# Query projection, load order and attention step order of a four-layer Perceiver kernel

## The chip, the cores and the metric

The kernel runs on one core of one Trainium2 chip. The metric is the device time of one execution in microseconds (us); the time shown for a kernel is the median of its runs.

The core's engines are named as in the profile: PE is TensorE (matrix products, into PSUM), DVE is VectorE, ACT is ScalarE, POOL is GpSimd and SP is SyncE, which here issues all loads. Each engine works through its own instructions in order.

## The reference

The model keeps a stream `x` of 2 x 256 tokens of width 256, and a context `ctx` of 2 x 4096 tokens of width 256 with a key mask. It runs eleven blocks, each on the layer norm of the stream and added to it:

```python
x = x + L0_xattn(layernorm(x), ctx, mask)   # 16 heads of 16, biases on q, k and v
x = x + L0_attn(layernorm(x))               # latent attention, 16 heads of 64, rotary
x = x + L0_ffn(layernorm(x))                # quantized, with a convolution of 3
x = x + L1_xattn(layernorm(x), ctx, mask)   # 16 heads of 16
x = x + L1_attn(layernorm(x))               # 16 heads of 16, over the stream itself
x = x + L1_ffn(layernorm(x))                # 16 experts, the best two
x = x + L2_xattn(ctx, layernorm(x))
x = x + L2_attn(layernorm(x))               # causal, gated
x = x + L2_ffn(layernorm(x))
x = x + L3_xattn(layernorm(x), ctx, ctx)    # linear attention with ranked features
x = x + L3_attn(layernorm(x))               # 16 heads of 16, in a window of 128
x = x + L3_ffn(layernorm(x))                # two layers
```

Four of these are touched: the two context attentions (`L0_xattn`, `L1_xattn`) and the two small attentions with heads of 16 (`L1_attn`, `L3_attn`). Such an attention is

```python
q, k, v = heads(h @ Wq + bq), heads(c @ Wk + bk), heads(c @ Wv + bv)
a = softmax(where(mask, -inf, q @ k.T) / 4)      # the scale differs by block
x = x + merge(a @ v) @ Wo
```

## The kernel before

Everything is kept transposed: features lie on the 128 partitions, and the 512 tokens along the row. A head of 16 takes 32 partitions (16 of its own, a row for the shift of the softmax, a row for the mask and empty ones), so a chunk of 128 partitions holds four heads, the 16 heads are four chunks `c`, and a *unit* is a chunk of one batch. There are eight units in an attention, with 256 queries each.

**PSUM.** A stage opens a pool of eight banks of 128 x 512 (`banks`, `stage`): by default two single ones called `mm`, two pairs called `sc` and two called `acc`. Both kinds of attention work with another split: one `mm`, three `sc` pairs, one `acc`. A tag with one buffer is given out again when its last reader is done.

**Start.** `constants` loads the vectors (biases and scales), `perceiver` loads x, and `context_constants` loads the mask, turns it into two rows of offsets that go to DRAM (`key_masks`), and computes `alive` (which batches have any unmasked key) with two products on PE. The weights of the first block, the features' weights and the first pair of context chunks (`ctx_k`) follow in the order of the code. SP issues these loads in the order that the scheduler gives them.

**Queries of a context attention** (`attend_to_context`, `take_queries`, `take`). The stream is centred (`xc`), four chunks are projected with `project`, which takes an `mm` bank for each; in between `measure` and `widen` make the reciprocal deviation of each token and spread it over all partitions (`wide`). For each chunk and batch DVE multiplies the projection by `wide` (L840) and adds the bias, in layer 1 also a factor 0 or 1 (L842, L844). Then the bank pool is changed and the attention starts. In it, step g computes first scores for unit g // 16 (L1113, L1121 takes their maxima), and later scores, exponentials and weighted sums (L1137, L1147, L1161), with projections of keys and values and the features of the last layer filled in by `plan`. In these two attentions the order of PE, DVE and ACT is written out by hand (`manual_schedule`); POOL and SP are ordered by the scheduler. The key tiles are filled with ones, since their mask and shift rows have to hold them; the value tiles `xv` too (POOL, L1071).

**A small attention** (`SmallAttention.attend`, L1405 on) does, in each step i, these things in order: sums and reciprocals of unit i-4 (`inverses`), the tops of unit i-1 transposed and added to its queries (`shift_queries`), first scores of unit i, weighted values of unit i-3 (`weigh`), second scores of unit i-1 (`scores`), and the product with the spread reciprocals of unit i-4 (`normalize`, by `to_heads`). Sums, tops and spread reciprocals (`den`) take turns in the one `mm` bank:

```python
if 0 <= i - 4 < n:
    self.inverses = self.net.inverses(self.weighed[i - 4])
if 0 <= i - 1 < n:
    self.shift_queries(i - 1)
if i < n:
    self.first_scores(i)
if 0 <= i - 3 < n:
    self.weigh(i - 3)
if 0 <= i - 1 < n:
    self.scores(i - 1)
if 0 <= i - 4 < n:
    self.normalize(i - 4)
```

Of the kernel before, what the change touches and what calls it, by code (L numbers as in the profile page):

```python
# [19 lines left out]
F32 = mybir.dt.float32  # L20
# [50 lines left out]
class Net:  # L71
# [87 lines left out]
    def constants(self):  # L159
        nc, const = self.nc, self.const  # L160
        c = lambda shape, name, dtype=F32: const.tile(shape, dtype, name=name, tag=name)
        self.vectors = c([P, sum(int(np.prod(v)) for v in VECTORS.values())], "vectors")
        nc.sync.dma_start(out=self.vectors, in_=self.ins["vectors"])
# [31 lines left out]
    def inverses(self, a):  # L195

        ps = self.mm("sums")
        for qt in range(2):
            self.matmuls(ps[:, qt * NG : (qt + 1) * NG], [(a[:, qt * P : (qt + 1) * P], self.den)])
        r = self.small.tile([P, 2, NG], F32, tag="inverses", name="inverses", bufs=2)  # L200
        self.nc.vector.reciprocal(r, ps[:, : 2 * NG].rearrange("p (q g) -> p q g", g=NG))
        return r

    def to_heads(self, r):

        ps = self.mm("den")
# [230 lines left out]
    def context_attention(self, x, q_bias, k_bias, v_bias, wq, wk, wv, wo, layer, alive=None, block=None):  # L437
# [11 lines left out]
        with tc.tile_pool(name="xa", bufs=1, reuse_waits="tile") as big, tc.tile_pool(name="xa_ctx", bufs=2, reuse_waits="tile") as cpool:  # L449
            a = ContextAttention(self, layer, big, cpool, (wk, k_bias), (wv, v_bias))  # L450
# [24 lines left out]
    def context_constants(self):  # L475
# [9 lines left out]
        with self.banks(), self.tc.tile_pool(name="mask", bufs=1, reuse_waits="tile") as tmp:  # L485
# [9 lines left out]
            most = tmp.tile([NR, 1], F32, name="mask_most", tag="mask_most")  # L495
            nc.vector.tensor_reduce(most, mf, AX.X, ALU.max)
            rows = tmp.tile([NR, NB, P], F32, name="batch_rows", tag="batch_rows")
            nc.gpsimd.memset(rows, 1.0)
            for b in range(NB):
                for sign, base in ((1, -b * NKC), (-1, b * NKC + NKC - 1)):  # L500
                    nc.gpsimd.affine_select(
                        out=rows[:, b, :],
                        in_=rows[:, b, :],
                        pattern=[[0, P]],
                        compare_op=ALU.is_ge,
                        fill=0.0,
                        base=base,
                        channel_multiplier=sign,
                    )
            self.alive = c([P, NB], "alive")  # L510
            ps = self.mm("alive_ps")
            for b in range(NB):
                nc.tensor.matmul(ps[:, b : b + 1], lhsT=rows[:, b, :], rhs=most, start=True, stop=True)
            nc.vector.tensor_scalar_min(self.alive, ps[:, :NB], 1.0)
# [265 lines left out]
class ContextAttention:  # L780
# [11 lines left out]
    def __init__(self, net, layer, big, cpool, keys, values):  # L792
        self.net, self.nc, self.layer, self.cpool = net, net.nc, layer, cpool
        (self.wk, self.k_bias), (self.wv, self.v_bias) = keys, values
        tile = lambda shape, name: big.tile(shape, F32, name=f"xa_{name}", tag=name)
        self.q = [tile([P, S], f"q{u}") for u in range(len(self.UNITS))]
# [4 lines left out]
        if layer == 0:  # L801
            for t in self.key_tiles:
                self.nc.gpsimd.memset(t, 1.0)
# [6 lines left out]

    def begin(self, n):

        self.begun = n
        if self.layer > 0:
            for t in self.key_tiles:
                self.nc.scalar.copy(t, self.net.ones[:, 0:1].to_broadcast([P, KC]))
            yield
# [4 lines left out]
    def take_queries(self, norm, wq, q_bias, alive):  # L822
        net = self.net
        for c in range(NC16):
            ps = net.project(wq, norm.chunks, c)
            if c == 0:
                net.measure(norm)
                waiting = ps
                continue
            if c == 1:  # L830
                wide = net.widened(norm.rstd)
                self.take(0, waiting, wide, q_bias, alive)
            self.take(c, ps, wide, q_bias, alive)

    def take(self, c, ps, wide, q_bias, alive):

        nc = self.nc
        for b in range(NB):
            q, at = self.q[b * NC16 + c], slice(b * S, (b + 1) * S)
            nc.vector.tensor_tensor(q, ps[:, at], wide[:, at], ALU.mult)  # L840
            if alive is None:
                nc.vector.tensor_scalar_add(q, q, q_bias[:, c : c + 1])  # L842
            else:
                nc.vector.tensor_scalar(q, q, q_bias[:, c : c + 1], alive[:, b : b + 1], ALU.add, ALU.mult)  # L844
# [131 lines left out]
    def attend(self, vpool, ppool, fpool):  # L976
# [12 lines left out]
        for g in range((n + 1) * PER + LAG + 2):  # L989
# [3 lines left out]
            run(self.beginning)  # L993
            run(fills.get(g, ()))
# [179 lines left out]
def l0_xattn(net, x):  # L1174
    wq, wk = net.load("L0x_wq", "L0x_wk")
    wv, wo = net.load("L0x_wv", "L0x_wo")
    qb, kb, vb = net.vec("L0x_qb"), net.vec("L0x_kb"), net.vec("L0x_vb")
    return net.context_attention(x, qb, kb, vb, wq, wk, wv, wo, 0)


def l0_attn(net, x):
# [9 lines left out]
    with tc.tile_pool(name="l0a", bufs=1, reuse_waits="tile") as big, tc.tile_pool(name="l0a_w", bufs=2, reuse_waits="tile") as work:  # L1191
# [36 lines left out]
        oT = big.tile([P, NCH, T], F32, name="oT", tag="oT")  # L1228

# [83 lines left out]
def l0_ffn_and_l1_xattn(net, x):  # L1313
# [4 lines left out]
        x, qb, None, None, wq, wk, wv, wo, 1, net.alive, block=lambda *of: l0_ffn(net, *of)  # L1318
# [17 lines left out]
class SmallAttention:  # L1336
# [68 lines left out]
    def attend(self):  # L1405
        n = len(self.UNITS)
        for i in range(n + 4):
            if 0 <= i - 4 < n:
                self.inverses = self.net.inverses(self.weighed[i - 4])
            if 0 <= i - 1 < n:  # L1410
                self.shift_queries(i - 1)
            if i < n:
                self.first_scores(i)
            if 0 <= i - 3 < n:
                self.weigh(i - 3)
            if 0 <= i - 1 < n:
# [911 lines left out]
```

## Time and profile before

| | before |
|---|---|
| median of 3 runs | 2512.33 us (2512.18 to 2951.45) |
| profiled execution | 2515.34 us, of which the span is 2513.4 us |
| granted PE clock in it | 0.958 |
| busy in the span | PE 93%, DVE 62%, ACT 43%, POOL 13% |
| loaded from DRAM | 154.25 MB |
| first small attention | about 1645 to 1704 us of the span |
| second small attention | about 2190 to 2244 us |
| context attention of layer 0, first scores | at 32.9 us |
| context attention of layer 1, first scores | at 957.6 us |

A row of the timeline gives start, duration, engine, line and operation (out <- in, sizes, how often), and in brackets how long the engine was idle before it and what ended that. A row of the chain gives start, length and owner of a piece of the work that ended last. `L180` is the helper behind most products, so its rows are told apart by the tiles' names. In the windows, the columns after the stretch are its length, the busy time and count of PE, PE's weight loads, DVE, ACT and POOL, then the granted clock, the share of the DMA engines and GB/s.

### The profile page before, as it was taken

How to read it: one execution, taken by the hardware profiler on the slowest of the kernel's cores; microseconds unless marked ns; L12 is line 12 of the kernel's file. 1: busy time of each engine (PE TensorE's matmuls, PEld its weight loads, DVE VectorE, ACT ScalarE, POOL GpSimd, SP SyncE). 2: the span in 40 equal slices, each digit the busy share in tenths (PEclk: the TensorE clock that was granted, in tenths of full speed). 3: DMA queues.
4: the chain of work that ended last, by engine and by line, in shares of the span. 5: the costliest groups of instructions: out<-in, count | busy, mean ns of one | idle time of the engine just before them, and what ended most of it. 6: DMA issues, size and time to landing. Idle time of an engine off the chain costs nothing.

```text
span 2513.4 us, 42846 instructions
## 1 busy us (share of the span) xinstructions
PE 2336.0 (93%) x17142; PEld 1252.9 (50%) x17142; DVE 1549.4 (62%) x2719; ACT 1093.2 (43%) x1917; POOL 333.2 (13%) x505
## 2 busy tenths in 40 slices
PE   7999999999999689999999999989999996889998
PEld 3455455544544364554454544554448453455454
DVE  4878888788736757877878778443241354334343
ACT  2456555555615333555555565531131252123232
POOL 3000001000024602000010000000011031002120
PEclk9999999999989799999999999989999997798989
DMA  5432232132010133322222220201232100100100
GB/s 185 138 105 86 88 96 94 52 111 64 10 38 35 48 103 108 101 91 90 90 94 86 77 98 28 83 14 43 96 100 93 43 18 14 34 21 12 58 12 21
DMA packets 97798, 174.42 MB, mean 69 GB/s; under 512 B 15120, under 2 KB 63888, under 8 KB 96704
## 3 DMA queue, kind: packets, MB, share of 16 engines
q1 hardware_dynamic: 97600, 171.68, 21.1%
q8 instruction: 136, 2.23, 0.4%
q14 instruction: 62, 0.51, 0.1%
HBM read 154.25 MB, written 0.59 MB: 62 GB/s over the span
## 4 chain that ended last, share of the span: by engine, by line
PE 57%; DVE 6%; ACT 2%; issue 1%; POOL 0%; DMA 0%; SPq 0%; ACTq 0%; DVEq 0%; POOLq 0%
PE s L1113 6%; PE s L1137 5%; PE proj L180 5%; PE attn_acc L1161 5%; PE v_ps L180 4%; PE expert L180 2%; PE k_ps L1034 2%; PE s L180 2%; PE c_acc L1753 2%; PE s L1430 2%; PE ffn_ps L180 2%; DVE mx L1121 2%; PE scores L342 1%; PE f_ps L180 1%; PE kc_sum L180 1%; PE qk_ps L180 1%
## 5 line engine op out<-in xcount | busy, mean ns | idle before, releaser
L1121 DVE TENSOR_REDUCE mx<-s 128x2 f32<-128x1024 f32 x512 | 603.2, 1221 | 224.6 <-PE s L1113 221.8
L1147 ACT ACTIVATE p<-s 128x1024 f32<-128x1024 f32 x512 | 496.0, 1021 | 255.8 <-PE s L1137 253.8
L1137 PE MATMUL s<-xa_q,xa_k 32*128 32x256 f32 x4096 | 342.3, 403 | 26.0 <-DVE mx L1121 23.0
L1113 PE MATMUL s<-xa_k,xa_q 32*128 32x512 f32 x2048 | 338.7, 642 | 7.0 <-ACT p L1147 2.3
L1137 PEld LDWEIGHTS s<-xa_q,xa_k 32*128 32x128 f32 x4096 | 212.7, 184 | 167.5 <-issue 92.6
L1161 PE MATMUL attn_acc<-p,xv 128*32 128x256 f32 x4096 | 276.2, 386 | 0.7 <-ACT p L1147 0.7
L1113 PEld LDWEIGHTS s<-xa_k,xa_q 32*128 32x128 f32 x2048 | 111.4, 183 | 124.7 <-issue 60.6
L667 DVE TENSOR_TENSOR ge<-fy 128x960 bf16<-128x960 f32 (+14 forms) x240 | 169.5, 706 | 6.5
L1161 PEld LDWEIGHTS attn_acc<-p,xv 128*32 128x32 f32 x4096 | 107.4, 109 | 131.4 <-issue 84.4
L621 POOL TENSOR_TENSOR fy<-fy,low 128x256 f32<-128x256 f32 x64 | 46.4, 725 | 881.3 <-ACT fy L620 881.1
L669 DVE TENSOR_TENSOR rank<-rank,ge 128x960 bf16<-128x960 bf16 (+14 forms) x240 | 104.2, 434 | 6.0
L671 DVE TENSOR_TENSOR rank<-rank,ge 128x960 bf16<-128x960 bf16 (+14 forms) x240 | 100.8, 420 | 2.6
L387 POOL TENSOR_SCALAR p<-p,r 128x128 f32<-128x128 f32 (+1 forms) x192 | 82.6, 442 | 127.0 <-DVE r L383 72.4
L1081 ACT COPY xv<-v_ps 128x512 f32<-128x512 f32 x64 | 37.6, 587 | 135.7 <-PE v_ps L180 135.7
L368 ACT ACTIVATE p<-p,top 128x256 f32<-128x256 f32 (+1 forms) x128 | 57.1, 447 | 66.6 <-DVE top L356 65.3
L180 PE MATMUL f_ps<-f_wk,f_ctx 128*128 128x256 f32 x256 | 68.9, 400 | 0.6 <-DMA f_ctx<-in_ctxT 0.6
L1034 PE MATMUL k_ps<-ctx_k,w_L0x_wq 128*64 128x512 f32 x256 | 66.0, 612 | 3.2 <-DMA ctx_k<-in_ctxT 2.9
L180 PE MATMUL v_ps<-w_L0x_wv,ctx_v 128*128 128x256 f32 x256 | 65.6, 400 | 0.8 <-ACT k_dense L1047 0.8
L180 PEld LDWEIGHTS f_ps<-f_wk,f_ctx 128*128 128x128 f32 x256 | 44.4, 189 | 43.3 <-issue 26.5
L1753 PE MATMUL c_acc<-pT,ctx_n 128*128 128x256 f32 x256 | 62.0, 387 | 4.2 <-ACT pT L1726 3.0
L180 PE MATMUL kc_sum<-f_tok,fy 128*128 128x257 f32 x256 | 64.2, 393 | 0.0
L180 PE MATMUL v_ps<-w_L1x_wv,ctx_v 128*128 128x256 f32 x256 | 63.8, 392 | 0.0
(478 smaller groups left out, 3366.8 us busy)
## 6 DMA issues: line engine op xcount, KB each, us to landing
ctx_k<-in_ctxT SPq DMA_DIRECT2D x128, 512.0 KB
ctx_v<-in_ctxT SPq DMA_DIRECT2D x64, 256.0 KB
xa_k<-k_dense SPq DMA_DIRECT2D x512, 32.0 KB
f_ctx<-in_ctxT SPq DMA_DIRECT2D x32, 256.0 KB
f_tok<-in_ctx SPq DMA_DIRECT2D x16, 512.0 KB
ctxT<-in_ctxT SPq DMA_DIRECT2D x16, 512.0 KB
ctx_n<-in_ctx SPq DMA_DIRECT2D x16, 512.0 KB
xa_k<-key_masks SPq DMA_DIRECT2D x128, 8.0 KB
```

The lines of the kernel that those rows point to most:

```text
L180: self.nc.tensor.matmul(out, lhsT=lhsT, rhs=rhs, start=i == 0, stop=i == len(pairs) - 1)
L387: nc.gpsimd.tensor_scalar(p[:, j, :nk], p[:, j, :nk], r[:, j : j + 1], 1.0, ALU.mult, ALU.mult)
L667: nc.vector.tensor_tensor(ge[:, :, :n], w[:, :, :n], w[:, :, P - n :], ALU.is_ge)
L669: nc.vector.tensor_tensor(rank[:, :, P - n :], rank[:, :, P - n :], ge[:, :, :n], ALU.add)
L671: nc.vector.tensor_tensor(rank[:, :, :n], rank[:, :, :n], ge[:, :, :n], ALU.subtract)
L1034: nc.tensor.matmul(ps[i * HR : (i + 1) * HR, :], lhsT=self.wk[:, d, c * HR : (c + 1) * HR], rhs=ctx[:, d, :], start=d == 0, stop=d == ND - 1,)
L1113: nc.tensor.matmul(pairs[i // 2][:, i % 2, :], lhsT=self.q[u][rows, qt * P : (qt + 1) * P], rhs=k[rows, :], start=True, stop=True,)
L1121: nc.vector.tensor_reduce(mx[:, qt, 2 * i : 2 * i + 2, kc], sc, AX.X, ALU.max)
L1137: nc.tensor.matmul(pairs[i // 2][:, i % 2, kk * S : (kk + 1) * S], lhsT=k[rows, at], rhs=self.q[u][rows, :], start=True, stop=True,)
L1147: nc.scalar.activation(p, sc, AF.Exp, scale=DH**-0.5)
L1161: nc.tensor.matmul(self.acc[i * HP : (i + 1) * HP, :S], lhsT=v[:, 2 * k2 + kk, at : at + HP], rhs=ps[i // 2][:, i % 2, kk * S : (kk + 1) * S],
L1753: nc.tensor.matmul(accs[m], lhsT=of[:, (k + i) % (KC // P), m * P : (m + 1) * P], rhs=pT[:, i, :], start=k + i == 0, stop=k + i == KT - 1,)
```

## The change

Three things change.

**Loads.** x is loaded first, then wk and wq, then the first pair of context chunks; the vectors, the mask, the features' weights and wv and wo follow. `alive` is found in the first self-attention block, not at the start. Four of the fourteen key tiles of layer 0 are filled by ACT at the start, and the other ten by POOL, as they are reached.

**Queries.** The four projections get banks of their own: two `mm` and the two halves of an `sc` pair. DVE finishes only unit 0. ACT copies the others out of PSUM as they are, and POOL multiplies them by `wide` and adds the bias, unit g at step g of the attention, while the scores of unit 0 run.

**Small attentions.** Tops and spread reciprocals share one bank, `aux`, half each, and the sums go into the second half of the bank of the weighted values, `acc`. The sums of unit i-3 come at the end of step i, and the product of unit i-4 before the second scores of unit i-1.

```diff
     def constants(self):
+        self.x = self.new_x()
+        nc.sync.dma_start(out=self.x, in_=self.ins["xT"])
         self.vectors = c([P, sum(int(np.prod(v)) for v in VECTORS.values())], "vectors")
-        nc.sync.dma_start(out=self.vectors, in_=self.ins["vectors"])
...
-    def inverses(self, a):
+    def inverses(self, a, ps=None):
-        ps = self.mm("sums")
+        ps = self.mm("sums") if ps is None else ps
...
-    def to_heads(self, r):
+    def to_heads(self, r, ps=None):
-        ps = self.mm("den")
+        ps = self.mm("den") if ps is None else ps
...
-            a = ContextAttention(self, layer, big, cpool, (wk, k_bias), (wv, v_bias))
+            a = ContextAttention(self, layer, big, cpool, (wk, k_bias), v_bias)
+            if layer == 0:
+                self.nc.sync.dma_start(out=self.vectors, in_=self.ins["vectors"])
+                self.context_constants()
+                self.focus = Focus(self)
+            a.wv, wo = values()
...
-        self.q = [tile([P, S], f"q{u}") for u in range(len(self.UNITS))]
+        self.queries = tile([P, NB, NC16, S], "q")
+        self.q = [self.queries[:, b, c] for b, c in self.UNITS]
+        self.wide = tile([P, T], "wide")
...
         if layer == 0:
-            for t in self.key_tiles:
-                self.nc.gpsimd.memset(t, 1.0)
+            self.fill_key_tiles(0, 4)
...
+    def fill_key_tiles(self, first, last):
+        for t in self.key_tiles[first:last]:
+            self.nc.scalar.copy(t, self.net.ones[:, 0:1].to_broadcast([P, KC]))
...
     def take_queries(self, norm, wq, q_bias, alive):
-        net = self.net
-        for c in range(NC16):
-            ps = net.project(wq, norm.chunks, c)
-            if c == 0:
-                net.measure(norm)
-                waiting = ps
-                continue
-            if c == 1:
-                wide = net.widened(norm.rstd)
-                self.take(0, waiting, wide, q_bias, alive)
-            self.take(c, ps, wide, q_bias, alive)
+        net, nc = self.net, self.nc
+        by_batch = lambda ap: ap.rearrange("p (b s) -> p b s", b=NB)
+        self.q_bias, self.alive = q_bias, alive
+        pair = net.sc("q_ps")
+        chunks = net.mm("q_ps"), net.mm("q_ps"), pair[:, 0], pair[:, 1]
+
+        def project(c, copied=True):
+            net.matmuls(chunks[c], [(wq[:, d, c * P : (c + 1) * P], of) for d, of in enumerate(norm.chunks)])
+            if copied:
+                nc.scalar.copy(self.queries[:, :, c], by_batch(chunks[c]))
+
+        project(0, copied=False)
+        net.measure(norm)
+        project(1)
+        project(2)
+        ps = net.widen(norm.rstd)
+        nc.scalar.copy(self.wide, ps)
+        project(3)
+        nc.vector.tensor_tensor(self.q[0], chunks[0][:, :S], self.wide[:, :S], ALU.mult)
+        self.add_bias(nc.vector, 0, 0)
+        nc.scalar.copy(self.queries[:, 1, 0], chunks[0][:, S:])
+
+    def add_bias(self, engine, b, c):
+        of, bias = self.queries[:, b, c], self.q_bias[:, c : c + 1]
+        if self.alive is None:
+            engine.tensor_scalar(of, of, bias, 1.0, ALU.add, ALU.mult)
+        else:
+            engine.tensor_scalar(of, of, bias, self.alive[:, b : b + 1], ALU.add, ALU.mult)
+
+    def finish_queries(self, u):
+        b, c = self.UNITS[u]
+        of = self.queries[:, b, c]
+        self.nc.gpsimd.tensor_tensor(of, of, self.wide[:, b * S : (b + 1) * S], ALU.mult)
+        self.add_bias(self.nc.gpsimd, b, c)
...
             run(self.beginning)
+            if 1 <= g < n:
+                self.finish_queries(g)
+            if self.layer == 0:
+                for t in self.key_tiles[4:][3 * g : 3 * g + 3]:
+                    nc.gpsimd.memset(t, 1.0)
...
 def l0_xattn(net, x):
-    wq, wk = net.load("L0x_wq", "L0x_wk")
-    wv, wo = net.load("L0x_wv", "L0x_wo")
+    wk, wq = net.load("L0x_wk", "L0x_wq")
...
         oT = big.tile([P, NCH, T], F32, name="oT", tag="oT")
+        net.find_alive()
...
     def attend(self):
         n = len(self.UNITS)
         for i in range(n + 4):
-            if 0 <= i - 4 < n:
-                self.inverses = self.net.inverses(self.weighed[i - 4])
+            aux = self.net.mm("aux") if 0 <= i - 1 else None
             if 0 <= i - 1 < n:
-                self.shift_queries(i - 1)
+                self.shift_queries(i - 1, aux[:, S:])
             if i < n:
                 self.first_scores(i)
             if 0 <= i - 3 < n:
                 self.weigh(i - 3)
+            if 0 <= i - 4 < n:
+                self.normalize(i - 4, aux[:, :S])
             if 0 <= i - 1 < n:
                 self.scores(i - 1)
-            if 0 <= i - 4 < n:
-                self.normalize(i - 4)
+            if 0 <= i - 3 < n:
+                self.inverses = self.net.inverses(self.weighed[i - 3], self.acc[:, S:])
```

`find_alive` holds what `context_constants` did for `alive` before: one memset and four selections on POOL, two products on PE, one DVE operation.

## The prediction

> **What bounds the kernel now.** I read the page's busy shares first, then its chain of work that ended last, then the timeline of the three places that the change touches, then the chain inside one of them, and the windows' clock last.
>
> ```profile
> PE 2336.0 (93%) x17142; PEld 1252.9 (50%) x17142; DVE 1549.4 (62%) x2719; ACT 1093.2 (43%) x1917; POOL 333.2 (13%) x505
> PE 57%; DVE 6%; ACT 2%; issue 1%; POOL 0%; DMA 0%; SPq 0%; ACTq 0%; DVEq 0%; POOLq 0%
> ```
>
> TensorE is busy 93% of the span and leads the chain, while GpSimd (POOL) is at 13% and nowhere on it. So 28 small operations put on POOL are cheap, and only places where PE waits can give time back. Three such places are touched. The start, and again the second context attention, in the timeline (start us, duration, engine, line):
>
> ```profile
> 12.45 1.29 DVE L232 TENSOR_TENSOR xc<-x,mean 128x512 f32<-128x512 f32 x2 [3.87 <-DMA ctx_k<-in_ctxT]
> 17.00 1.98 PE L180 MATMUL proj<-xc,w_L0x_wq 128*128 128x512 f32 x4
> 25.67 5.37 PE L180 MATMUL proj<-xc,w_L0x_wq 128*128 128x512 f32 x8 [1.95 <-DVE xa_q L840]
> 32.29 0.40 DVE L840 TENSOR_TENSOR xa_q<-proj,wide 128x256 f32<-128x256 f32 x1
> 32.90 1.98 PE L1113 MATMUL s<-xa_k,xa_q 32*128 32x512 f32 x8 [1.86 <-POOL xv L1071]
> ...
> 942.12 1.98 PE L180 MATMUL proj<-xc,w_L1x_wq 128*128 128x512 f32 x4 [0.78 <-DVE xc L232]
> 957.62 1.14 PE L1113 MATMUL s<-xa_k,xa_q 32*128 32x512 f32 x8 [1.75 <-issue]
> ```
>
> The third and fourth projections wait 1.95 us for VectorE (DVE) to empty the two "mm" banks, and the first scores start only after DVE has read the last projection (32.29 + 0.40 = 32.69, scores at 32.90). The releaser named there, a POOL memset, has nothing to do with the scores; the pool of banks changes hands at this point, so the last reader of the old banks is the one that counts. From first projection to first scores: 15.9 us in layer 0, 15.5 us in layer 1.
>
> The small attentions: the chain of waits in order of time through one steady step (start, length, owner).
>
> ```profile
> 1678.25 0.59 PE sums L180 x4
> 1678.86 0.22 DVE inverses L201
> 1679.13 0.44 PE top_ps L1467 x2
> 1679.57 1.08 PE s L1430 x16
> 1680.64 1.00 PE attn_acc L1485 x16
> 1681.64 1.45 PE s L1430 x16
> 1683.09 0.62 PE den L209 x16
> 1683.80 0.43 DVE sa_oT L1500
> 1684.23 0.14 issue
> 1684.37 0.59 PE sums L180 x4
> ```
>
> A step lasts 1684.37 - 1678.25 = 6.12 us, and PE, DVE, PE, DVE take turns in it: one bank ("mm") holds sums, tops and denominators in turn, so PE stands still 0.30 us for the reciprocal and 0.70 us for the product. The second scores take 1.45 us where the first take 1.08, since they reach their second pair of banks before DVE has reduced it.
>
> **The change, part by part.** Lengths are those of the rows above or named.
>
> 1. Start, loads. The queue SP now issues x, wk, wq and both ctx_k ahead of vectors, mask, f_wk, wv and wo: 0.52 + 0.26 + 0.52 + 1.05 = 2.36 MB. The DMA slices of the first 15 us move about 350 GB/s, from about 2.1 us on, so ctx_k is there at about 8.8 (before: the matmuls on it began to run freely at 15.14), vectors at 9.4, the mask at 9.6. This has a price: DVE is in order, and in the built program the mask's four operations stand ahead of xc. They took from 5.46 to 7.26 = 1.8 us, so xc starts at about 9.6 + 1.8 = 11.4, not 12.45: only 1.05 us of it is seen there. k_ps (about 2.7 us from 8.8 on) is over at 11.5 and no longer stands ahead of the first projection, which before waited for it until 17.00. Projection 0 goes at 12.1, as xc's first half ends. On SP the copies of key_masks now stand between ctx_k and the k_dense copies; with the mask's round trip (masks at 11, written at about 13) and eight or ten issues of 0.65 us the first key tile is complete near 20, before it is wanted.
> 2. Queries (both layers). Each layer loses 14 of 16 DVE operations (0.42 and 0.35 to 0.41 us) and gets four ScalarE (ACT) copies (128x512 out of PSUM: 0.58 us, L269; the half: 0.37, L1493) and 14 POOL operations. Four chunks have banks of their own (two mm, one sc pair), so no projection waits. PE's order, with steps read from starts in the timeline: proj 1.8, var 1.7, proj 1.7, proj 1.7, widen 1.0, proj 1.7 = 9.6 us; then 0.2 for the drain, copy 0.58 and half copy 0.37: first scores 10.8 us after the first projection, by my estimate. DVE's query 0 is done earlier (wide, 0.42, 0.35). Layer 1: 942.1 + 10.8 = 952.9 against 957.6: **-4.7 us**. Layer 0: 12.1 + 10.8 = 22.9, and I add 1.1 for a cold PE (the first scores took 1.98 us there against 1.14 in layer 1): 24.0 against 32.9: **-8.9 us**, bounds -6 to -10.
> 3. The 14 operations on POOL: seven of 725 ns (128x256 product, L621) and seven of 478 ns (128x256 scalar, L387) = 8.4 us per layer. Unit 1 is wanted 16 steps of some 3 us later, so they hide behind unit 0's scores. In the built order the first xv memset stands behind six of them (4 x 0.73 + 2 x 0.48 = 3.9 us), and ACT's copy of the first values waits for it: wide at 950.7 in layer 1, xv ready at about 955.7, wanted when v_ps ends at 955.9. Cost zero to 0.5 us. The key tiles' fill (ten memsets of 0.52 us on POOL, four on ACT) is over before the first keys land, as before.
> 4. A rule that speaks against part 2. The row first: the same 128x256 DVE add took 353 ns, and 829 ns while POOL's xv memsets ran (L842). The Trainium skill, "SBUF — State Buffer", section on who interferes with whom, says that VectorE and GpSimd share one port pair as an exclusive lock, held for a whole instruction. POOL's first product starts with wide, just as DVE finishes query 0: by the rule DVE's 0.35 us becomes up to 1.1, by the quiet row 0.35. By both query 0 is ready before or with the last ACT copy 2 us later, so the sum stays; the reductions that follow read PSUM. I take 0, upper end 0.7 per layer.
> 5. Alive moves into the first self-attention block: four PE matmuls (0.98 us cold for four, L513) and a 0.16 us DVE operation in a PE-bound stage: **+0.5 us**, bounds 0 to 1. At the start its absence lets mean go as soon as x lands; that is inside part 1.
> 6. Small attentions. Per step PE now does tops, first scores, weigh, den, second scores, sums without a wait between: 0.37 + 1.08 + 1.00 + 0.57 + 1.08 + 0.52 = 4.62 us by start-to-start times. What would be late next: DVE has 0.42 + 2.36 + 0.42 + 0.21 = 3.41 us; the next tops need the product, which ends at about 4.4 us of the step (reductions start 1.18 us behind the scores, take 2.36, then 0.42), so 0.2 us of slack remains. I take 4.7: (6.12 - 4.7) x 4 full steps = 5.7. The step without new first scores (1690.49 to 1696.79, 6.3 us) comes to 3.6 by the same terms; its weigh and scores ran cold (1.71 and 1.99), so I count 1.8 of 2.7. First block: **-7.5 us**. Second block (with the band, 6.99 us a step): 0.54 us of band matmuls twice, 5.7 a step, 5.1 over four; and 1.0 for the last: **-6.1 us**. The first steps and the three tail steps stay: there weigh follows sums directly and waits 0.3 us for the reciprocal, in exchange for the 0.7 us of the product.
> 7. A rule on that. The row: den reaches the shared bank 2.1 us behind the tops, and the DVE add that reads their half lasts 0.42. The Trainium skill, "PSUM — Partial Sum Buffer", section on bank collisions, wants two engines kept apart by bank and quadrant, not by address: halves of one bank are not independent. By the rule sums must wait for ACT's copy out of acc's other half, and weigh for the reciprocal. In full steps den and second scores (1.65 us) cover copy and drain (0.37 + 0.14), and tops and first scores cover the reciprocal: 4.7 by either. In the tail, 3 x 0.3 us: in part 6 already. A schedule that waited openly at both would cost some 0.8 us x 10 = 8 us, the upper end.
>
> **Sum.** -8.9 - 4.7 + 0.5 - 7.5 - 6.1 = -26.7 us. Against the profiled execution, 2515.3 us (span 2513.4 and 1.9 around it), that is 2488.6; it stood 3.0 us above the median 2512.3 of the three runs, so the median comes to **2486 us**. That is 1.1%; the verdict and about what a measurement of this kernel can tell from no change is 2%, or 50 us.
>
> **Rivals.**
> - *The start gives little* (chance 0.17). vectors, mask and wv are behind 2.4 MB, DVE's xc behind them, and SP's key copies behind the mask's round trip. For it: SP and DVE are in order, and xc gains only 1 us. Against: the keys have 4 us to spare. If first scores come at 31, 2486 + 7 = 2493.
> - *The small attentions turn to another wait* (0.15). With one aux and one acc bank, tops wait for DVE's product and sums for ACT's copy. For it: 0.2 us of slack. If a step stays at 5.6 and 6.5: 2486 + 0.9 x 4 + 0.8 x 4 + 1.5 = 2494.
> - *Slower: the PE clock* (0.05). Place: the two context attentions, 1370 us at a granted clock of 0.98 and 1.00. If less idle time or a shifted phase lets the throttle take 0.02 of it, PE's share costs about 27 us and the rest of the gain goes; from 0.02 down it decides, 0.025 gives about 2520. For it: small dips are in the page. Against: the dips lie where PE idles, which the windows show:
>
> ```profile
> 958.00:1615.00 657.00, 640.64 (x6041) 329.32 (x6034) 518.01 (x737) 370.22 (x568) 62.84 (x90) 1.00 0.26 83
> 1646.00:1667.00 21.00, 17.14 (x135) 10.22 (x136) 11.10 (x13) 6.72 (x8) 0.00 (x0) 0.67 0.12 37
> ```
>
> The column behind the five engines is the clock: 1.00 in the dense stretch, 0.67 in the beginning of the small attention.
> - *It gains over 2%* (0.03): only if the warmer PE also halves the cold stretches around each place and the scores' steps shorten too, 2460.
>
> **Numbers.** Forecast 0.60. Range 2473 to 2503: down to all upper ends of the gains with some 6 us of warmer clock, up to both partial rivals with some us of scatter. Faster by over 2% 0.03, within 2% 0.94, slower by over 2% 0.03 (the clock rival mostly ends inside 2%).
>
> **What would show it.** First context scores near 24 us (not 33) and about 11 us after layer 1's first projection; xc behind mask_most on DVE; POOL's products beside the first reductions; small-attention steps of 4.7 and 5.7 us with no wait of PE for DVE's reciprocal or product in full steps. Wrong if the first scores wait for an xa_k copy or for ACT, if steps stay near 6, or if a stretch that was not touched changes.

## The result, and the profile after

The changed kernel took 2491.01 us (median of four executions, 2486.71 to 2496.69), the kernel before 2512.61 us beside it (2512.2 to 2512.9 without the one disturbed execution of 2951). The ratio is 0.9883, with a 95% interval of 0.9851 to 0.9914: faster by 1.2%, clear of no change and under 2%. 2486 was forecast, with a range of 2473 to 2503. In four later series the kernel before had medians of 2516 to 2519 us, and the changed one, which ran in two of them, 2492.5 and 2492.7; so times below are compared within one series only, and where a series has no run of the changed kernel, gains over the kernel before are compared.

The page's busy shares and the shares of its chain, of the changed kernel: almost the same picture as before. TensorE stays the bound. POOL has gained 24 instructions and 15 us; of its 1% of the chain nearly all is in lines that the change leaves as they are (L389, L535 to L539).

```profile
PE 2332.9 (94%) x17142; PEld 1253.6 (50%) x17142; DVE 1532.3 (61%) x2691; ACT 1099.7 (44%) x1929; POOL 348.2 (14%) x529
PE 56%; DVE 5%; ACT 3%; POOL 1%; issue 1%; DMA 0%; ACTq 0%; SPq 0%; DVEq 0%; POOLq 0%
```

The timeline of the changed kernel at the start and at the second context attention (start us, duration, engine, line; in brackets the idle time before and who ended it):

```profile
11.43 0.24 DVE L1873 TENSOR_SCALAR mu_rest<-vectors 128x2 f32<-128x2 f32 x2 [9.15 <-DMA vectors<-in_vectors]
14.91 1.28 DVE L234 TENSOR_TENSOR xc<-x,mean 128x512 f32<-128x512 f32 x2 [1.48 <-DMA key_masks<-masks]
16.25 1.98 PE L181 MATMUL q_ps<-xc,w_L0x_wk 128*128 128x512 f32 x4 [1.73 <-DVE xc L234]
27.06 1.14 PE L1149 MATMUL s<-xa_k,xa_q 32*128 32x512 f32 x8 [0.95 <-ACT xa_q L861]
...
936.92 1.98 PE L181 MATMUL q_ps<-xc,w_L1x_wq 128*128 128x512 f32 x4 [0.78 <-DVE xc L234]
947.73 1.14 PE L1149 MATMUL s<-xa_k,xa_q 32*128 32x512 f32 x8 [0.95 <-ACT xa_q L861]
```

From first projection to first scores it is 27.06 - 16.25 = 10.81 us in layer 0 and 947.73 - 936.92 = 10.81 us in layer 1, where 10.8 was forecast (in `e4_after`, the same kernel again, 10.81 too; in `e11_after` 12.50, with half clock from 16.06 to 19.47). But xc and the first projection come at 14.91 and 16.25, where 11.4 and 12.1 were forecast.

The chain of waits through one step of the first small attention and into its tail (start, length, owner): PE's pieces follow one another without a gap, 1672.65 - 1667.84 = 4.81 us a step against 6.12 before. Only in the tail DVE's reciprocal stands between.

```profile
1667.84 1.49 PE s L1469 x16
1669.33 1.00 PE attn_acc L1524 x16
1670.33 0.44 PE aux L211 x16
1670.77 1.08 PE s L1469 x16
1671.84 0.54 PE attn_acc L181 x4
1672.38 0.28 PE aux L1505 x2
1672.65 1.49 PE s L1469 x16
...
1676.48 0.81 issue
1677.29 0.22 DVE inverses L203
```

**How far ahead the changed kernel is, from place to place.** I laid PE's instructions of two traces side by side and took the difference of the starts of the same instruction. Three traces of the changed kernel (the first, and the two yardsticks below) against the trace of before, us:

| place (us in the trace of before) | forecast | first trace | e4_after | e11_after |
|---|---|---|---|---|
| first scores, layer 0 (33) | -8.9 | -5.84 | -6.57 | -4.70 |
| what is left of it at 96 | -8.9 | -4.45 | -7.31 | -5.55 |
| layer 1, change from 935 to 958 | -4.7 | -4.69 | -4.68 | -4.69 |
| first small attention, change from 1667 to 1711 | -7.5 | -7.87 | -8.00 | -7.91 |
| second small attention, change from 2201 to 2250 | -6.1 | -6.61 | -6.51 | -6.52 |

Three of the four parts stand within about 0.5 us of the forecast in every trace. The start does not, and it is the one that differs from trace to trace. All differences are against one trace of before.

**What of layer 1 is the clock.** `e1_small`, below, has the old queries too. Here are the third and fourth projections of before, with the window around them, and then the same place in `e1_small`:

```profile
950.50 5.37 PE L180 MATMUL proj<-xc,w_L1x_wq 128*128 128x512 f32 x8 [2.01 <-DVE xa_q L840]
942.10:957.70 15.60, 11.82 (x44) 6.40 (x44) 7.11 (x18) 4.84 (x7) 1.71 (x2) 0.89 0.09 37
```

```profile
938.51 1.98 PE L180 MATMUL proj<-xc,w_L1x_wq 128*128 128x512 f32 x4 [0.78 <-DVE xc L233]
946.89 3.67 PE L180 MATMUL proj<-xc,w_L1x_wq 128*128 128x512 f32 x8 [2.01 <-DVE xa_q L841]
952.32 1.14 PE L1114 MATMUL s<-xa_k,xa_q 32*128 32x512 f32 x8 [1.75 <-issue]
938.50:952.40 13.90, 10.13 (x44) 5.82 (x45) 7.11 (x18) 4.83 (x7) 1.71 (x2) 1.00 0.10 38
```

In `e1_small` it is 952.32 - 938.51 = 13.81 us from first projection to first scores, in before 15.50. The 1.7 us between them are the clock, 0.89 against 1.00: before has a stretch of half clock from 951.25 to 954.66, `e1_small` has none here. At full clock the new queries give 13.81 - 10.81 = 3.0 us in layer 1, not 4.69. No trace with the new queries has half clock there; whether the waits of the old order bring it on, two traces cannot tell.

**The loss after the first scores.** PE's waits for the context's transfers, timeline of the changed kernel:

```profile
36.25 1.93 PE L1070 MATMUL k_ps<-ctx_k,w_L0x_wk 128*64 128x512 f32 x6 [1.30 <-DMA ctx_k<-in_ctxT]
55.95 1.96 PE L181 MATMUL f_ps<-f_wk,f_ctx 128*128 128x256 f32 x8 [1.77 <-DMA f_ctx<-in_ctxT]
74.95 1.04 PE L1070 MATMUL k_ps<-ctx_k,w_L0x_wk 128*64 128x512 f32 x2 [1.60 <-DMA ctx_k<-in_ctxT]
76.16 1.93 PE L1070 MATMUL k_ps<-ctx_k,w_L0x_wk 128*64 128x512 f32 x6 [0.17 <-DMA ctx_k<-in_ctxT]
```

They are 4.84 us. In the timeline of before the same four are 0.25 + 0.59 + 0.50 + 0.46 = 1.80 us:

```profile
42.69 1.93 PE L1034 MATMUL k_ps<-ctx_k,w_L0x_wq 128*64 128x512 f32 x6 [0.25 <-DMA ctx_k<-in_ctxT]
61.20 1.97 PE L180 MATMUL f_ps<-f_wk,f_ctx 128*128 128x256 f32 x8 [0.59 <-DMA f_ctx<-in_ctxT]
79.10 1.04 PE L1034 MATMUL k_ps<-ctx_k,w_L0x_wq 128*64 128x512 f32 x2 [0.50 <-DMA ctx_k<-in_ctxT]
80.61 1.93 PE L1034 MATMUL k_ps<-ctx_k,w_L0x_wq 128*64 128x512 f32 x6 [0.46 <-DMA ctx_k<-in_ctxT]
```

At the second scores the changed kernel is 7.49 us ahead (it also runs these first scores with a warm PE, 1.14 us against 1.98), and 7.49 - (4.84 - 1.80) = 4.45 is what is left at 96 us. An earlier start is thus partly handed to the next transfer. In the other two traces these waits come to 2.75 and 2.65 us, and what the first scores gained is still there at 96 us.

**Untouched stretches.** Near 2120 us, in code that the change does not touch, the first trace loses 3.3 us. The timeline of before, then of the changed kernel, shows the same eight matmuls:

```profile
2140.07 4.89 PE L180 MATMUL proj<-yT,w_L3x_wq 128*128 128x512 f32 x8 [0.46 <-ACT yT L219]
```

```profile
2121.58 6.51 PE L181 MATMUL proj<-yT,w_L3x_wq 128*128 128x512 f32 x8 [0.46 <-ACT yT L221]
```

The difference of 1.62 us is the granted clock: over the 17 us from 2140 on it was 0.93 before, and 0.75 over the 19 us from 2121 on after. In the clock records of all these traces, half clock comes in stretches of 3.4 us and multiples of it (but for the last, cut by the end), so one stretch more costs a dense piece 1.7 us. The Trainium skill, "TensorE: Matmul & The Clock Gate", Part 1, says that the clock is decided in windows of 3.4 us that run free of the program; the stretches agree with it.

### The profile page after: what moved, and what is told of

Same layout as the page of the kernel before. It is cut to its first block, busy times and chain, and to the rows that moved or that the text cites. A ratio compares the mean times of both kernels' runs of the same rounds, so it can differ in the third digit from the quotient of the medians.

```text
span 2494.6 us, 42805 instructions
## 1 busy us (share of the span) xinstructions
PE 2332.9 (94%) x17142; PEld 1253.6 (50%) x17142; DVE 1532.3 (61%) x2691; ACT 1099.7 (44%) x1929; POOL 348.2 (14%) x529
## 4 chain that ended last, share of the span: by engine, by line
PE 56%; DVE 5%; ACT 3%; POOL 1%; issue 1%; DMA 0%; ACTq 0%; SPq 0%; DVEq 0%; POOLq 0%
PE s L1149 6%; PE s L1173 5%; PE proj L181 5%; PE attn_acc L1197 5%; PE v_ps L181 4%; PE expert L181 2%; PE k_ps L1070 2%; PE s L181 2%; PE c_acc L1792 2%; PE s L1469 2%; PE ffn_ps L181 2%; DVE mx L1157 2%; PE kq_ps L181 1%; PE f_ps L181 1%; PE kc_sum L181 1%; PE qk_ps L181 1%
## 5 line engine op out<-in xcount | busy, mean ns | idle before, releaser
L389 POOL TENSOR_SCALAR p<-p,r 128x128 f32<-128x128 f32 (+1 forms) x192 | 83.1, 446 | 128.5 <-DVE r L385 74.5
L1070 PE MATMUL k_ps<-ctx_k,w_L0x_wk 128*64 128x512 f32 x256 | 66.8, 616 | 5.3 <-DMA ctx_k<-in_ctxT 5.0
L181 PEld LDWEIGHTS f_ps<-f_wk,f_ctx 128*128 128x128 f32 x256 | 44.4, 189 | 44.5 <-issue 26.5
```

Source lines behind the costliest of these rows:

```text
L181: self.nc.tensor.matmul(out, lhsT=lhsT, rhs=rhs, start=i == 0, stop=i == len(pairs) - 1)
L389: nc.gpsimd.tensor_scalar(p[:, j, :nk], p[:, j, :nk], r[:, j : j + 1], 1.0, ALU.mult, ALU.mult)
L1070: nc.tensor.matmul(ps[i * HR : (i + 1) * HR, :], lhsT=self.wk[:, d, c * HR : (c + 1) * HR], rhs=ctx[:, d, :], start=d == 0, stop=d == ND - 1,)
```

## The experiments

### Which part gives what

`e1_small`: the kernel before, with nothing of the change but the new order of the small attentions.

> The kernel before with the new order of the two small attentions alone. Theory A, the parts add up and each stays where it is: the two attentions give what they gave in the trace of after, 8.6 and 6.6 us, so about 2512.5 - 15 = 2497.5, with 4.8 and 5.7 us a step and nothing moved ahead of 1645 us. Rival B, the steps are only faster because the stretch ahead of them changed (another phase of the clock): the steps stay above 5.5 us in this kernel, and the time stays above 2504.

Measured: 2499.44 us against 2518.96, ratio 0.9914 (0.9882 to 0.9945). In its trace the two attentions give 7.87 and 6.82 us, with steps of 4.8 us: A, and these parts don't depend on the rest of the change. (Ahead of them the trace has moved as well, 2.5 us at 1660, though nothing is changed there; the stretch of half clock that it lacks in layer 1 is part of that.) The 19.5 us between the medians are more than the 14.7 of the two places; the interval, 14 to 30 us, holds both.

`e2_queries`: the kernel before with the new queries, all fourteen key tiles still filled on POOL at once.

```diff
-        self.q = [tile([P, S], f"q{u}") for u in range(len(self.UNITS))]
+        self.queries = tile([P, NB, NC16, S], "q")
+        self.q = [self.queries[:, b, c] for b, c in self.UNITS]
+        self.wide = tile([P, T], "wide")
...
+            if 1 <= g < n:
+                self.finish_queries(g)
```

> The kernel before with the new queries alone (four banks, copies on ACT, POOL finishes units 1 to 7); the order of loads, alive and the small attentions as before. Theory A, the start's gain comes from the queries and what the loads win is given back to the context transfers by 80 us: first scores near 28 us (17.0 + 10.8) against 32.9, a shift of about -4.5 us left at 100 us, another -4.7 in layer 1, so about 2503. Rival B, the loads carry the start: a shift of at most -2 at 100 us, about 2506.

Measured: 2518.83 against 2518.96, ratio 1.000 (0.9985 to 1.0016). Layer 1 gives its 4.69 us; the first scores of layer 0 come at 33.60, later than the 32.90 of before, so neither A nor B as I had put them. The timeline tells why; first `e2_queries`, then POOL's rows in the kernel before:

```profile
3.30 6.85 DVE L1852 TENSOR_SCALAR mu_rest<-vectors 128x2 f32<-128x2 f32 x2 [3.30 <-DMA vectors<-in_vectors]
3.60 6.52 POOL L805 MEMSET xa_k<- 128x512 f32 x14
5.10 5.32 DVE L489 CAST mask_f<-mask_i 16x512 f32<-16x512 int32 x1
33.60 1.14 PE L1131 MATMUL s<-xa_k,xa_q 32*128 32x512 f32 x8 [1.00 <-DMA f_ctx<-in_ctxT]
```

```profile
8.44 0.34 POOL L799 MEMSET xa_top<- 128x128 f32 x2 [5.09 <-PE alive_ps L513]
8.72 6.52 POOL L803 MEMSET xa_k<- 128x512 f32 x14
```

Two 128x2 operations of DVE stand from 3.30 to 10.15, and POOL's row of memsets ends at 10.12. The mask is late by 4.5 us, SP holds the first ctx_k behind the mask's write (12.56 instead of 8.02), and the rest follows. In the kernel before the same memsets began at 8.72, behind a wait for the product for alive, when the mask was done. That the new layout of the queries freed them from this wait is my reading; the trace shows only that it is gone. The gain after 958 us is lost too: from 1102 us to the end this trace falls back from 6.48 us ahead to 2.29 us behind, 8.8 us in code that is the same as before. The clock covers that: from there on its records have 162 us at half clock, those of before 142, and 20 us more at half clock cost a dense piece 10 us. The medians leave room for a gain of 3.8 us at most, which the 3.0 us of layer 1 at full clock fit and 4.69 do not.

`e5_act_fill`: the same, with one line changed.

```diff
             for t in self.key_tiles:
-                self.nc.gpsimd.memset(t, 1.0)
+                self.nc.scalar.copy(t, self.net.ones[:, 0:1].to_broadcast([P, KC]))
```

> As e2_queries (before with the new queries alone), but the fourteen key tiles are filled on ACT and none on POOL. Theory L, the lock: in e2_queries DVE's mu_rest and mask_f stood from 3.30 to 10.15 us because POOL's memsets of key tiles ran back to back in that stretch; without them the mask is ready near 7.3 as in before, the projections start near 16.5 to 17.5 and the first scores come at 27.5 to 28.5 us instead of 33.6, about 5 us earlier in all. Rival D, the data were late (the transfers): mu_rest and mask_f end near 10 again and the first scores stay near 33.

Measured: 2506.0 against 2516.19, ratio 0.9959 (0.9943 to 0.9974).

```profile
2.10 7.36 ACT L805 COPY xa_k<-ones 128x512 f32<-128x512 f32 x14
3.47 0.24 DVE L1852 TENSOR_SCALAR mu_rest<-vectors 128x2 f32<-128x2 f32 x2 [3.47 <-DMA vectors<-in_vectors]
5.50 0.41 DVE L489 CAST mask_f<-mask_i 16x512 f32<-16x512 int32 x1 [1.79 <-DMA mask_i<-in_mask]
29.16 1.14 PE L1131 MATMUL s<-xa_k,xa_q 32*128 32x512 f32 x8 [0.95 <-ACT xa_q L846]
```

L, the lock: with POOL out of the way the same two DVE operations take 0.24 us, the mask is ready at 7.3, and the first scores come 4.4 us earlier than in `e2_queries` (a little later than expected, since the first k_ps ran at 4.72 us, with waits, before the projections). At 96 us it is 6.22 us ahead of before. With layer 1's 4.7 (3.0 at full clock) that is 10.9 us (9.2), and the medians give 10.2, with an interval of 6.5 to 14.3.

`e3_old_loads`: the changed kernel, with the loads of the start in the old order.

```diff
+        nc.sync.dma_start(out=self.vectors, in_=self.ins["vectors"])
...
-    wk, wq = net.load("L0x_wk", "L0x_wq")
+    wq, wk = net.load("L0x_wq", "L0x_wk")
+    wv, wo = net.load("L0x_wv", "L0x_wo")
```

> The changed kernel with the loads at the start in the order of before (stream, vectors, mask, wq and wk, wv and wo, then the keys); all else as changed. Theory A: as fast as the changed kernel within 1 us (about 2490), since after the first scores the transfers of the context decide. Rival B, loading the keys first is worth what the first scores gain by it: 3 to 4 us slower than the changed kernel, about 2494.

Measured: 2498.67, and 2492.47 for the changed kernel in the same series: B, 6.2 us slower by the medians. The intervals overlap (0.9883 to 0.9941 and 0.9861 to 0.9916), but the trace says the same: the first scores come at 33.14, and at 96 us it is 1.9 us behind the kernel before. The order of loads isn't the whole of it, though: here too DVE stands (mask_f from 5.44 to 8.62, until POOL's memsets end at 8.33), and `e5_act_fill`, also with the old order, is as far ahead at 96 us (6.2) as the changed kernel (4.5 to 7.3). By this reading, loading the keys first pays because the vectors then arrive only after POOL's memsets are over, and because the ctx_k no longer waits behind the mask.

`e4_after` and `e11_after`: the changed kernel again, as yardsticks.

> The changed kernel once more, for a second trace and as the yardstick of this call. About 2491 median. If the two untouched stretches near 2130 and 2290 us that lost 3.3 and 2.9 us in its first trace lost them to the phase of the clock, these losses are gone or stand elsewhere in this trace, each as a multiple of 1.7 us (half of a stretch of 3.4 us at half clock); if the change makes them, they come again in the same places.

> The changed kernel once more, as the yardstick of this call: 2490 to 2493 by the medians so far, and first scores near 26.5 us.

Measured: 2492.47 against 2518.96, ratio 0.9889 (0.9861 to 0.9916); 2492.72 against 2518.71, ratio 0.9904 (0.9888 to 0.9919). "Gone or elsewhere" was too simple: both traces lose again at the two places (2.2 and 4.2 us in `e4_after`, 3.1 and 2.9 in `e11_after`), and not all losses are multiples of 1.7 us. But the change doesn't make it: at the first place (2140 to 2166 in the trace of before) `e2_queries` loses 3.3 us and `e5_act_fill` none, and both run there exactly what the kernel before runs. At the second (2312 to 2345) every kept trace loses 2.9 us or more, these two included: there it is the one trace of before that ran fast. The first is a place where PE idles and the clock drops, and how many stretches of 3.4 us it takes differs from one execution to the next.

### What holds the start

`e12_mask_space`: the changed kernel, with the mask's tiles in memory that xc does not take over.

```diff
-                self.context_constants()
+                self.context_constants(big)
...
-    def context_constants(self):
+    def context_constants(self, tmp):
...
-        with self.tc.tile_pool(name="mask", bufs=1, reuse_waits="tile") as tmp:
+        if True:
```

> The changed kernel with the mask's three tiles in the pool that lives through the whole context attention, so that xc no longer takes over memory that the write of key_masks still reads; nothing else is moved. Theory A: the wait of xc for that write (1.48 us in the first trace of the changed kernel) goes; xc follows mask_most directly, at about 13.4, the first projection follows k_ps at about 14.6 instead of 16.25, and the first scores come 1.5 us earlier, near 25.5; at 100 us under 1 us of it is left. Rival B: the wait stays, since it was for something else (a transfer on the same queue), or the first scores don't move, since the key tiles decide.

Measured: 2500.16 against 2518.49, ratio 0.9928 (0.9911 to 0.9945), 18.3 us faster, where the changed kernel is 21.6 to 26.5 us faster in its series. The intervals overlap, but at 96 us its trace is 1.1 us behind the kernel before, 5.6 to 8.4 us worse than the changed kernel. Its timeline:

```profile
13.09 1.26 DVE L234 TENSOR_TENSOR xc<-x,mean 128x512 f32<-128x512 f32 x2
14.41 3.39 PE L181 MATMUL q_ps<-xc,w_L0x_wk 128*128 128x512 f32 x4 [1.86 <-DVE xc L234]
26.91 1.14 PE L1149 MATMUL s<-xa_k,xa_q 32*128 32x512 f32 x8 [0.95 <-ACT xa_q L861]
62.80 3.56 PE L181 MATMUL f_ps<-f_wk,f_ctx 128*128 128x256 f32 x8 [9.29 <-DMA f_ctx<-in_ctxT]
```

The wait of xc was for that memory: it goes, and xc and the first projection come when A said. But the projection then ran at half clock (3.39 us for four matmuls instead of 1.98), and the first scores came at 26.91, amid the 26.33 to 28.20 of the three traces of the changed kernel. And an effect that neither theory had: PE stands 9.29 us at 62.8. The issue on SP shows the cause, first in the changed kernel, then here:

```profile
50.67 0.60 SPq L737 DMA_DIRECT2D f_ctx<-in_ctxT  x1
```

```profile
59.49 1.30 SPq L737 DMA_DIRECT2D f_ctx<-in_ctxT  x2
```

SP's order is not written by hand; the scheduler had placed this load behind further copies of key tiles.

`e6_mask_late`: vectors loaded second, the mask's operations behind xc and in other memory.

```diff
+            norm = self.mask_rows(self.center, self.halves(x))   # xc first, then the mask
+            a.wv, wo = wo()
```

> The changed kernel with the vectors loaded second, the mask's four DVE operations placed behind xc, and their tiles in memory that xc does not take over. Theory A: xc starts near 8 to 9 us instead of 14.9, the first projection right behind k_ps at about 15 instead of 16.25, the first scores near 25.5 instead of 27.06; but the transfers of the context decide after that, so at 100 us no more than 1 us of it is left. Rival B: the first scores decide, and the whole 1.5 us is left at 100 us.

Measured: 2497.6 against 2516.19, ratio 0.9924 (0.9892 to 0.9956). xc at 8.71, first projection at 14.12, first scores at 24.93 (7.97 us ahead of before, close to the forecast's 24.0), 9.50 us ahead at 50 us, and 1.2 at 96: again the second half of f_ctx, issued at 55.96, for which PE stands 8.19 us. So A's conclusion holds, but by another load than I thought.

`e7_ctx2`: the changed kernel with two pairs of ctx_k buffers.

```diff
-            ctx = self.cpool.tile([P, ND, KC], F32, name=f"ctx_k{i}", tag=f"ctx_k{i}", bufs=1)
+            ctx = self.cpool.tile([P, ND, KC], F32, name=f"ctx_k{i}", tag=f"ctx_k{i}", bufs=2)
...
         self.load_keys_ctx()
+        self.load_keys_ctx()
```

> The changed kernel with two pairs of ctx_k buffers instead of one, the second pair loaded at once. Theory A, after the first scores the layer-0 attention is held by its context transfers (PE waits 1.30 us at 36 for ctx_k, 1.77 at 56 for f_ctx, 1.77 at 75 for ctx_k, 4.8 in all): the two ctx_k waits go, and at 100 us the kernel stands 2 to 3 us ahead of the changed kernel, some 2 us less in all. Rival B, the queue of SP and the rate of the transfers decide and not the number of buffers: the waits move to ctx_v or f_ctx and at 100 us the gain is under 1 us, or the first scores come later, since the second pair lands ahead of the mask.

Measured: 2497.0 against 2516.19, ratio 0.9916 (0.9885 to 0.9948). Both theories saw a part: the ctx_k waits are gone, but vectors land at 13.93 behind the second pair, and the first scores come at 31.14. At 96 us it is 5.99 us ahead of before, no more than the changed kernel.

`e8_all`: `e6_mask_late`, two pairs of ctx_k (the second behind the mask), and the first projection ahead of the first k_ps.

> A version meant to beat both: e6_mask_late with the two pairs of ctx_k buffers and with the first projection placed ahead of the first k_ps on PE. Theory A: first projection near 9.5 us, first scores near 23 us, no waits for ctx_k behind it, 5 to 7 us ahead of the changed kernel at 100 us and about that in all (2485). Rival B: the chain from the mask to the first key tile (k_ps to 14, copies by SP of 0.6 us each, landing 2 us later) holds the first scores at 25 us or later, and the gain is 2 us.

Measured: 2495.53 against 2516.19, ratio 0.9918 (0.9889 to 0.9947). First scores at 24.17, 11.60 us ahead at 50 us, 1.46 at 96: PE stands 10.34 us for the second half of f_ctx. Neither rival named that.

`e9_f_ctx` and `e10_f_ctx_alone`: the halves of f_ctx loaded two ahead, on top of `e8_all` and of the changed kernel.

```diff
         self.load()
+        self.load()
...
-            if t % 2 == 0:
-                self.load()
...
+            if t % 2 == 1:
+                self.load()   # behind the matmuls of this half
```

> e8_all with both halves of the first f_ctx loaded at the start of the context attention, and each later half behind the matmuls of the one two ahead of it. In e8_all PE stood 10.34 us at 59 us for the second half, since the scheduler had put its issue on SP behind two key tiles' copies (issued at 55.0, against 50.7 in the changed kernel). Theory A: this wait goes, and the 11.6 us by which e8_all led the trace of before at 50 us are still there at 100 us: some 4 us more than the changed kernel (7.3 in the last trace), about 4 us less in all than the changed kernel of this call. Rival B: another transfer (ctx_v, the next f_ctx or the key copies) holds PE there, and it is level with the changed kernel.

> The changed kernel with only the edit of the f_ctx loads. Theory A: its waits for f_ctx go (1.77 us in the first trace, 0.59 in the second), those for ctx_k stay and take over part of it: 0 to 1 us less than the changed kernel. Rival B: the earlier load delays the ctx_k pair behind it on SP by 0.7 us: no gain.

Measured: `e9_f_ctx` 2485.04 (ratio 0.9869, 0.9848 to 0.9890), `e10_f_ctx_alone` 2490.12 (0.9888, 0.9874 to 0.9903), the changed kernel 2492.72 (0.9904, 0.9888 to 0.9919), all against 2518.71. In the timeline of `e9_f_ctx` PE has no wait for a transfer left between the first scores and 100 us:

```profile
23.83 1.24 PE L1159 MATMUL s<-xa_k,xa_q 32*128 32x512 f32 x8 [0.95 <-ACT xa_q L871]
27.75 1.99 PE L182 MATMUL v_ps<-w_L0x_wv,ctx_v 128*128 128x256 f32 x8 [0.81 <-ACT k_dense L1093]
55.98 1.13 PE L1159 MATMUL s<-xa_k,xa_q 32*128 32x512 f32 x4 [0.47 <-DVE mx L1167]
```

It is 14.64 us ahead of before at 96 us, against 5.55 for the changed kernel in this series: theory A, with more than its 4 us. It is 7.7 us faster than the changed kernel by the medians. The two intervals overlap a little (0.9888 to 0.9890), but the slowest of its five runs (2490.39) is ahead of the fastest of the changed kernel's five (2491.66). Against the kernel before it is 33.7 us faster. `e10_f_ctx_alone` gives 2.6 us by the medians with overlapping intervals, its f_ctx wait gone and one ctx_k wait longer (1.66): undecided.

## Why the prediction was right, and where it was not

- **Step 1, the start's loads: wrong.** xc at 11.4 was forecast, 14.91 came, 3.5 us later. Two terms failed. First, I let the transfers land one after another in the order of their issue: ctx_k at 8.8, vectors at 9.4. By 10.0 us the trace had moved 2.84 MB (41, 375, 346 and 375 GB/s in four pieces of 2.5 us), more than the 2.36 MB I counted up to ctx_k, and yet the second ctx_k was wanted until 10.9 and the vectors until 11.43: later loads share the bandwidth with earlier ones. The mask landed at 11.61 instead of 9.6, which is 2.0 us of the 3.5. Second, xc waited 1.48 us for the write of key_masks, which `e12_mask_space` shows to be for memory. I had also not seen that an operation of a much later block (mu_rest, L1873) stands ahead of the mask on DVE, but it cost nothing here: the mask came 0.2 us behind the vectors that mu_rest waits for.
- **Step 2, the queries: right in the mechanism, lucky in a size.** 10.81 us in both layers, and 4.69 us in layer 1 (4.7 forecast). But the 15.5 us that I set against 10.8 hold a stretch of half clock, which I did not look for: 1.7 of the 4.69 us are that stretch, and 3.0 are the queries. The layer-0 row of 5.37 us that I showed is slow for the same reason (half clock from 26.24 to 29.66). The layer-0 gain of 8.9 became 5.84, 6.57 and 4.70 by the first scores; what is missing comes from step 1, and in `e11_after` 1.7 us of it from half clock during the projections. My 1.1 us for a cold PE was not needed (the first scores took 1.14 us). That "the keys have 4 us to spare" was true of the first key tile only; the next ctx_k, f_ctx and ctx_k take back up to 3.0 us.
- **Step 3, POOL's operations: right.** They hide. What I passed over was POOL's other work: the ten memsets of key tiles start at 2.2 us and would hold DVE if the vectors came earlier, as the `e2_queries` and `e5_act_fill` pair shows.
- **Step 4, the shared port: right in sum.** DVE's second operation on query 0 took 0.46 us beside POOL's products in layer 1, against 0.41 before; 0 was taken, up to 0.7 allowed. By the rule it could have been 1.1 us; these products did not hold it. Memsets did, elsewhere, and for longer than the rule says: 6.6 us in `e2_queries`.
- **Step 5, alive: right.** Four matmuls take 0.60 us at 764.7 (0.98 counted), and the first trace loses 0.53 us there.
- **Step 6, the small attentions: right, a little low.** Steps of 4.81 us (4.7) and, in the second, of 5.69 and 5.97 (5.7); 7.9 and 6.5 us in all, where 7.5 and 6.1 were forecast. The first scores take 1.49 us in a step, not 1.08. DVE's reductions do not hold them up (the last one before ends at 1666.52). A part of them starts at 1668.20, right after the first of ACT's two exponentials of the scores before, of 1.02 us each, has ended at 1668.14, and so in twelve full steps of three traces. Two shorter pieces (0.44 us for den, 0.28 for tops) give about half of the 0.41 us back: 4.81 us against my sum of 4.62, in which I had asked only when DVE would be late. As forecast, the tail waits for the reciprocal (0.22 us in the chain).

```profile
1667.12 1.94 ACT L1513 ACTIVATE p<-s 128x1024 f32<-128x1024 f32 x2 [1.17 <-PE s L1469]
```

- **Step 7, halves of one bank: right.** No full step waits at sums or weigh; only the tail does.
- **The rivals.** "The start gives little" came in half, by its named cause: vectors and mask behind the keys. "The small attentions turn to another wait" did not come beyond the 0.2 us of step 6: steps of 4.81 and 5.69 to 5.97 us, not 5.6 and 6.5. A gain of over 2% did not come. The clock rival failed where it was placed: the dense stretch shows 1.00 again.

```profile
948.00:1605.00 657.00, 640.66 (x6041) 329.31 (x6038) 517.46 (x736) 371.54 (x570) 71.02 (x102) 1.00 0.27 83
```

The sum of the parts as measured is -5.8 (mean of three at 96 us) - 4.7 + 0.5 - 7.9 - 6.5 = -24.4 us against -26.7. The medians differ by 21.6, 26.5 and 26.0 us in three series. So 2.3 us of the forecast gain were not there: the start is 3.1 us short, the small attentions give 0.8 more. What is left of the 5 us between 2486 and 2491 is within the scatter of the clock's stretches, and I can't assign it further. That two of the series come within 1 us of 26.7 is luck: without the half clock in the trace of before, the parts add up to 22.7.

## What to carry to other kernels

Count a start by what each in-order queue holds ahead of the first useful operation, including work that a scheduler has moved up from a later block, and let loads share the bandwidth instead of landing in turn. An earlier start is only kept if the following loads are issued earlier too: look for the next waits for a transfer, and fix SP's order or prefetch one buffer further before anything else. When a whole program moves by some microseconds, compare place by place, since stretches that nobody touched can shift the sum by 3 to 9 us with the clock, and look for half clock at the place itself in both traces: here it was 1.7 us of a gain of 4.7.

## What the hardware showed that I had not expected

- In `e2_queries` POOL's memsets of 0.52 us start every 0.46 us, so in the profile they overlap, and two 128x2 operations of DVE that take 0.24 us together without them stood for 6.85 us, until 0.03 us after the last of fourteen. The Trainium skill, "SBUF — State Buffer", section on who interferes with whom, speaks of a lock held for one whole instruction; here DVE was not let in between two of them. I take it that the overlap is why, which no run here separates. Not every DVE operation is stopped: in the kernel before, xc, which takes one input from PSUM, took 0.69 and 0.68 us in the midst of the same memsets.
- Moving the mask's three tiles to other memory (`e12_mask_space`) cost 9.29 us of PE's time at a place 48 us later, through the scheduler's order on SP.
